# Layer 0's attention scores as one-pass products of halves, two units in a batch

## The chip, the cores and the metric

The kernel runs on one core of a Trainium2 chip. The metric is the time of one execution in microseconds of device time, median over runs; a profile is one further execution recorded by the hardware profiler, and its span is the time from its first to its last instruction. The engines are TensorE (PE: matmuls; PEld is its weight load), VectorE (DVE), ScalarE (ACT), GpSimd (POOL) and SyncE (SP, which here issues nearly all DMA transfers, in program order).

## The reference

The input is `x`, 8 images of 384 channels by 32 x 32 pixels. Two layers follow each other; the change is in layer 0 alone, an attention over the 1024 pixels of each image with 8 heads of 48 channels and a bias that depends on the distance of two pixels:

```python
tokens = x.reshape(b, c, n).transpose(0, 2, 1)
qkv = (tokens @ qkv_w + qkv_b).reshape(b, n, 3, NUM_HEADS, HEAD_DIM)
qkv = jnp.transpose(qkv, (2, 0, 3, 1, 4))
q, k, v = (qkv[0], qkv[1], qkv[2])
scale = HEAD_DIM ** (-0.5)
attn = jnp.einsum('bhnd,bhmd->bhnm', q * scale, k)
attn = attn + _relative_bias(h, w, mlp_w1, mlp_b1, mlp_w2, mlp_b2)[None]
attn = jax.nn.softmax(attn, axis=-1)
out = jnp.einsum('bhnm,bhmd->bhnd', attn, v)
out = out.transpose(0, 2, 1, 3).reshape(b, n, c)
out = out @ proj_w + proj_b
```

Layer 0 is `x + conv_attention(group_norm(x))`. Layer 1, an attention with 6 heads and a feed-forward part with sign weights, takes its output token by token; nothing in it changes.

## The kernel before

**Order of work.** `_layer0` (L275) runs image after image. For each image the attention's 32 units are followed by the projection of the next image to its queries, keys and values. A scheduler isn't used: every engine runs the instructions in the order in which the Python code writes them, and a small list, `_Later` (L69), runs small pieces of side work a given number of units later. SP's transfers wait in one queue: a transfer whose data isn't there holds back all behind it. The built program gives them eight completion semaphores in turn.

**Pairs.** The 8 heads are 4 pairs. A head pair takes 128 partitions, two halves of 64 rows (`S0`), of which a head fills 48 (`D0`). The 16 rows left over in pairs 0 to 2 (`FR` each) carry the heads of pair 3 (`NF0`): the projection makes three tiles of 128 rows, and six 16-row transfers a side (L680) collect pair 3's rows into its own tile.

**Projection** (`Ahead`, L624). The product with the weights is cut into three one-pass products of parts (`xh` high, `xl` low, `xd` mixed; type fp32r) instead of one four-pass fp32 product; the weights' parts `wc` are read from DRAM in blocks of 576 KB (`_Cut.load`, L161). There are six blocks (`BLOCKS`: 3 pairs, queries or keys), each 18 matmuls of 128x128 by 512. `take` (L666) puts a block's two PSUM tiles together: ACT scales and shifts one (L671), DVE adds the other (L675). After the third block `project_v` makes the values (L700, L708, L712). The order of the six blocks alternates between images, so that three of six weight blocks are already in SBUF for the next image.

**Attention.** A unit is a head pair, 512 of the queries and 256 of the keys. `scores` (L741) makes eight fp32 matmuls on four 64x64 tiles of PE (rows by head, columns by half of the keys), into two PSUM tiles; DVE adds the bias out of PSUM (L759), ACT takes the exponential (L763). `weigh` (L769), two units later (`LAG`), multiplies the exponentials with the values, also in 64x64 tiles, accumulating four units in one PSUM tile; ACT copies its first part (L787) and DVE adds the second (L790). A row of ones beside the values gives the sums. `divide` (L796) sends the sums through DRAM, POOL takes their reciprocals as a power (L808), and `rd`, `rb` (L812, L820) spread them; POOL multiplies (L824). For pair 3 six transfers then move rows back under pairs 0 to 2 (L834). At unit 3 of the next image `project_out` (L860) multiplies with the output weights (`pp`, L847) and adds the residual `res` (L863).

**PSUM.** One pool of four tiles of two banks (`mm2`) serves everything; a tile that is allocated waits until the earliest freed one has been read.

**Beside the units.** Loading the next image, its statistics (`group_norm`), masks of its high parts (`xm`, in the `qk` tiles) and their rounding to `xh`, and cutting layer 1's weights into parts (images 1 to 3) are placed at fixed units.

Of the kernel before, what the change touches and what calls it, by code (L numbers as in the profile page):

```python
# [101 lines left out]
BLOCKS = [(pair, s) for pair in range(KC) for s in range(2)]  # L102
BLOCKS1 = [(0, 1), (0, 0), (1, 1), (2, 1), (1, 0), (2, 0)]
# [171 lines left out]
def _layer0(tc, ins, x1, sums, shared, weights, beside):  # L275
# [9 lines left out]
    with ExitStack() as ctx:  # L285
        const = ctx.enter_context(tc.tile_pool(name="a_const", bufs=1))
        qkp = ctx.enter_context(tc.tile_pool(name="a_qk", bufs=NP0))
# [273 lines left out]
        def project_qk(b, xn):  # L561

            qk = {
                pair: qkp.tile([P, 2, N], F32, tag="qk", name=f"qk{b}_{pair}") for pair in range(NP0)
            }
            for pair in range(NF0):
                t = qk[pair]
                for s in range(2):
                    pq = mm2(f"pq{b}_{pair}_{s}")
# [11 lines left out]
                    if s == 0:  # L581
                        nc.vector.tensor_scalar(
                            t[:, s], flat2(pq), bias, D0**-0.5, ALU.add, ALU.mult
                        )
                    else:
                        nc.scalar.activation(t[:, s], flat2(pq), AF.Identity, bias=bias)
                    later.step()
                for j in range(2):
                    nc.sync.dma_start(
                        qk[NF0][j * S0 + pair * FR : j * S0 + (pair + 1) * FR],  # L590
                        t[j * S0 + D0 : (j + 1) * S0],
                    )
            return qk

        BB = len(BLOCKS) // 2
# [28 lines left out]
        class Ahead:  # L624
# [4 lines left out]
            def __init__(self, b, xn):  # L629
                self.b, self.xn = b, xn  # L630
                self.qk = {}
                self.parts, self.ps = [[], [], []], {}

            def tile(self, pair):
                if pair not in self.qk:
                    self.qk[pair] = qkp.tile([P, 2, N], F32, tag="qk", name=f"qk{self.b}_{pair}")
                return self.qk[pair]

            def high(self, k):
                return self.tile(k // 2)[:, k % 2]  # L640

            def mask(self, k):
                _masked(nc, self.high(k), self.xn[:, k])

            def round(self, k):
                t = etile(f"xh{self.b}_{k}", dtype=F32R)
                nc.scalar.copy(t, self.high(k))
                self.parts[0].append(t)

            def low(self, k):  # L650
                t = etile(f"xl{self.b}_{k}", dtype=F32R)
                nc.vector.tensor_sub(t, self.xn[:, k], self.high(k))
                self.parts[1].append(t)

            def mixed(self, k):
                t = etile(f"xd{self.b}_{k}", dtype=F32R)
                _mixed(nc, t, self.parts[1][k].bitcast(F32), self.high(k))
                self.parts[2].append(t)

            def products(self, cuts, n, i):  # L660
                if (n, i // 2) not in self.ps:
                    pair, s = BLOCKS[n]
# [3 lines left out]
            def take(self, n):  # L666
                pair, s = BLOCKS[n]
                t = self.tile(pair)[:, s]
# [9 lines left out]
                last = self.tile(NF0)  # L678
                for j in range(2):
                    nc.sync.dma_start(  # L680
                        last[j * S0 + pair * FR : j * S0 + (pair + 1) * FR, s],
                        t[j * S0 + D0 : (j + 1) * S0],
                    )
                later.step()

# [55 lines left out]
        def scores(b, qk, u, weigh):  # L741
            pair, h, m2 = u
            s = [mm2(f"s{b}_{pair}_{h}_{m2}_{j}") for j in range(2)]
            for i in range(2):
                for c in range(2):
                    for j in range(2):
                        rows = slice(j * S0, j * S0 + D0)
                        nc.tensor.matmul(  # L748
                            s[j][ts(c, QP), i], qk[pair][rows, 1, ts(4 * m2 + 2 * i + c, QP)],
                            qk[pair][rows, 0, ts(h, HALF)], start=True, stop=True,  # L750
# [18 lines left out]
        def weigh(b, u, es):  # L769
# [24 lines left out]
            return finish  # L794

# [131 lines left out]
        for k, at in enumerate(((17, 22, 23), (21, 25, 26), (27, 30, 31))):  # L927
            for when, stage in zip(at, cut_weights_v(k)):
                later.after(when + 1, stage)
        for b in range(B):  # L930
            held = []
            for i, u in enumerate(units):
                done = held.pop(0) if len(held) == LAG else None
                held.append(
                    (u, scores(b, qk, u, lambda: weigh(b, *done) if done else None))
                )
                if i == (16 if b == 0 else 1) and b + 1 < B:
                    xn = load(b + 1)
                    for at, stage in zip(
                        (2, 3, 4, 6, 9, 10, 11) if b == 0 else (5, 6, 7, 10, 13, 13, 13),  # L940
# [3 lines left out]
                if i == 3 and b > 0:  # L944
                    project_out(b - 1, residuals(b - 1, etile), range(NF0))
# [5 lines left out]
                if i == 28 and b == 0:  # L951
                    cuts = _Cut(
                        nc, cut, BLOCKS,
                        shared.pool.tile([P, KC * 3 * C], F32R, tag="w", name="wc"),
# [3 lines left out]
                if b in (1, 2, 3) and i == 12:  # L958
                    t = cut_tile(f"cw{b}")
                    weights.load_part(b - 1, t)  # L960
                    for at, stage in enumerate(
                        weights.cut(
                            b - 1, t, lambda name, b=b, t=t: t if name == "cl" else cut_tile(f"{name}1{b}")
                        )
                    ):
                        later.after(4 + at, stage)
                masks, rounds = ((28, 29, 31), ()) if b == 0 else ((25, 26, 27), (28, 29, 30))
                if b + 1 < B:
# [4 lines left out]
                    if i in rounds:  # L973
                        ahead.round(rounds.index(i))

            def weigh_held():
                finish = weigh(b, *held.pop(0))
                if finish is not None:
                    finish()

            if b + 1 == B:
                while held:
                    weigh_held()
                break
            order = [n % len(BLOCKS) for n in range(b % 2 * BB, b % 2 * BB + len(BLOCKS))]

            if b == 0:
                wh = const.tile([P, KC, C], F32R, tag="wv", name="wvh")
                nc.sync.dma_start(wh.bitcast(F32), cut_v[:, 0])
# [1383 lines left out]
```

## Time and profile before

| | |
|---|---|
| median of 3 runs | 2942.41 us (2942.0 to 2945.76) |
| the profiled execution | 2940.6 us |
| its span | 2939.1 us, mean granted PE clock 0.999 |
| one image, from its projection to the end of its attention | 853.5 to 1019.4 us: 165.9 us, PE busy 165.9, DVE 113.0, ACT 80.2, POOL 26.0 |
| one image later in its cycle, 725.6 to 891.5 us | 165.9 us, PE busy 165.9 |
| HBM read / written | 161.83 / 40.28 MB |

In the busy-time table, the time of the matmuls is a union: several that run side by side count once, and their ends are modelled, so the distance from start to start tells more than a duration. fp32 matmuls leave two records each, one-pass ones a single record. The idle time behind a group names the engine that ended it. In the windows' table each stretch has the busy time of each engine and the number of its instructions.

### The profile page before, as it was taken

How to read it: one execution, taken by the hardware profiler on the slowest of the kernel's cores; microseconds unless marked ns; L12 is line 12 of the kernel's file. 1: busy time of each engine (PE TensorE's matmuls, PEld its weight loads, DVE VectorE, ACT ScalarE, POOL GpSimd, SP SyncE). 2: the span in 40 equal slices, each digit the busy share in tenths (PEclk: the TensorE clock that was granted, in tenths of full speed). 3: DMA queues.
4: the chain of work that ended last, by engine and by line, in shares of the span. 5: the costliest groups of instructions: out<-in, count | busy, mean ns of one | idle time of the engine just before them, and what ended most of it. 6: DMA issues, size and time to landing. Idle time of an engine off the chain costs nothing.

```text
span 2939.1 us, 47521 instructions
## 1 busy us (share of the span) xinstructions
PE 2913.6 (99%) x19538; PEld 1703.0 (58%) x19538; DVE 1969.8 (67%) x1999; ACT 1504.5 (51%) x1846; POOL 493.5 (17%) x318
## 2 busy tenths in 40 slices
PE   8999999999999999999999999999999999999998
PEld 3465665657575666634546647647647647655553
DVE  3976758586676757573655775875875875875756
ACT  2644636264444636363643655555555555564644
POOL 3121202021110202012202202302302302311020
PEclk9999999999999999999999999999999999999999
DMA  7642131413122130323311212112112112112111
GB/s 191 197 147 84 50 111 46 121 45 98 47 74 73 39 113 24 100 69 107 78 56 31 84 31 72 67 32 72 67 32 72 67 32 72 67 40 83 40 46 39
DMA packets 131970, 214.35 MB, mean 73 GB/s; under 512 B 62144, under 2 KB 81072, under 8 KB 130368
## 3 DMA queue, kind: packets, MB, share of 16 engines
q1 hardware_dynamic: 128480, 209.39, 24.3%
q8 instruction: 157, 2.57, 0.4%
q10 hardware_dynamic: 3264, 1.82, 0.2%
q14 instruction: 69, 0.57, 0.1%
HBM read 161.83 MB, written 40.28 MB: 69 GB/s over the span
## 4 chain that ended last, share of the span: by engine, by line
PE 92%; DVE 3%; DMA 2%; ACT 2%; issue 1%; SPq 0%; POOL 0%; DVEq 0%; ACTq 0%
PE s L748 15%; PE o L779 15%; PE s L1725 11%; PE o L1774 10%; PE pg L170 6%; PE y2p L2019 6%; PE y1p L1968 5%; PE pp L847 4%; PE pv L1662 4%; PE pm L170 3%; PE pp L1871 3%; PE vg L700 2%; PE pq L1514 2%; PE pq L572 1%; DMA rb<-rd 1%
## 5 line engine op out<-in xcount | busy, mean ns | idle before, releaser
L763 ACT ACTIVATE e<-e 128x1024 f32<-128x1024 f32 x512 | 534.5, 1057 | 333.2 <-DVE e L759 316.7
L759 DVE TENSOR_TENSOR e<-s,grow 128x1024 f32<-128x1024 f32 x512 | 601.1, 1218 | 154.6 <-PE s L748 137.8
L748 PE MATMUL s<-qk 48*64 48x512 f32 x4096 | 606.4, 590 | 1.8 <-DVE e L759 1.8
L779 PE MATMUL o<-e,v 64*64 64x512 f32 x4096 | 603.5, 589 | 0.0
L1736 ACT ACTIVATE e<-s,kc 128x512 f32<-128x512 f32 x768 | 463.3, 693 | 173.5 <-PE s L1725 163.9
L1725 PE MATMUL s<-qk,qk 64*64 64x512 f32 x3072 | 419.4, 592 | 1.6 <-DVE oT L1784 1.3
L1774 PE MATMUL o<-e,v 64*64 64x512 f32 x3072 | 415.0, 590 | 0.0
L748 PEld LDWEIGHTS s<-qk 48*64 48x64 f32 x4096 | 231.7, 132 | 235.3 <-issue 98.7
L779 PEld LDWEIGHTS o<-e,v 64*64 64x64 f32 x4096 | 251.6, 133 | 188.4 <-issue 97.3
L1725 PEld LDWEIGHTS s<-qk,qk 64*64 64x64 f32 x3072 | 154.3, 132 | 191.5 <-issue 109.0
L1751 DVE TENSOR_TENSOR t<-t,e 128x1024 f32<-128x1024 f32 x192 | 230.9, 1221 | 45.6 <-ACT e L1736 45.4
L1774 PEld LDWEIGHTS o<-e,v 64*64 64x64 f32 x3072 | 160.5, 133 | 168.2 <-issue 141.9
L808 POOL TENSOR_TENSOR inv<-sums,over 128x16 f32<-128x16 f32 x32 | 95.8, 2992 | 843.9 <-DMA sums<-sd 776.8
L1955 DVE TENSOR_REDUCE parts<-y 128x1 f32<-128x1024 f32 x75 | 89.7, 1217 | 102.6 <-ACT y L1952 102.1
L1748 DVE TENSOR_TENSOR t<-e,e 128x1024 f32<-128x1024 f32 x96 | 114.0, 1224 | 58.8 <-ACT e L1736 58.7
L1631 POOL TENSOR_TENSOR hc<-hc,rsqrt 128x32 f32<-128x32 f32 x24 | 136.7, 5696 | 2.0
L1662 PE MATMUL pv<-wv,bx 128*128 128x384 f32 x384 | 128.3, 491 | 0.0
L1871 PE MATMUL pp<-oT,L_attn_proj_wT 128*128 128x512 f32 x288 | 126.3, 595 | 1.9 <-DVE oT L1837 1.8
L847 PE MATMUL pp<-oT,wp 128*128 128x512 f32 x288 | 125.7, 595 | 0.0
L1662 PEld LDWEIGHTS pv<-wv,bx 128*128 128x128 f32 x384 | 119.4, 314 | 9.8 <-ACT e L1736 4.1
L675 DVE SCALAR_TENSOR_TENSOR qk<-pg,qk 128x1024 f32<-128x1024 f32 x42 | 51.4, 1225 | 100.3 <-PE pg L170 74.2
L1968 PE MATMUL y1p<-lun,w 128*128 128x512 f32 x360 | 113.5, 396 | 3.0 <-DVE lun L1918 3.0
(225 smaller groups left out, 3583.8 us busy)
## 6 DMA issues: line engine op xcount, KB each, us to landing
rb<-rd SPq DMA_DIRECT2D x110, 256.0 KB
wc<-there SPq DMA_DIRECT2D x25, 576.0 KB
wc<-cut SPq DMA_DIRECT2D x24, 576.0 KB
xn<-in_x_dram SPq DMA_DIRECT2D x24, 512.0 KB
res<-in_x_dram SPq DMA_DIRECT2D x24, 512.0 KB
x<-res SPq DMA_DIRECT2D x24, 512.0 KB
bx<-x SPq DMA_DIRECT2D x8, 1536.0 KB
rq<-hi SPq DMA_DIRECT2D x48, 256.0 KB
```

Source lines behind the costliest of these rows:

```text
L170: self.nc.tensor.matmul(out[:, h], w[:, i, k], part[k][:, ts(h, HALF)], start=(k == 0 and i != 1), stop=(k == KC - 1 and i != 0),)
L748: nc.tensor.matmul(s[j][ts(c, QP), i], qk[pair][rows, 1, ts(4 * m2 + 2 * i + c, QP)], qk[pair][rows, 0, ts(h, HALF)], start=True, stop=True,)
L759: nc.vector.tensor_add(e.rearrange("p (i q) -> p i q", i=2), s[j], bass.AP(near.tensor, near.offset, [near.ap[0], [-QROWS * IW, 2], [1, HA ...
L763: nc.scalar.activation(e, e, AF.Exp)
L779: nc.tensor.matmul(po[ts(j, S0), r], v[keys, 2 * m2 + i, 2 * pair + j, :], es[j][keys, ts(i, HALF)], start=(m2 == 0 and i == 0), stop=(m2 ...
L847: nc.tensor.matmul(pps[b, m][:, h], (wp[:, k] if k < NF0 else wl)[:, ts(m, P)], oT[:, k, ts(h, HALF)], start=(k == 0), stop=(k == (NF0 if ...
L1662: nc.tensor.matmul(pv[:, i, 0:C], xt[:, k].rearrange("c (p m) -> c m p", m=MT)[:, 2 * m2 + i], wv[:, k], start=(k == 0), stop=(k == KC - 1),)
L1725: nc.tensor.matmul(s[j][ts(c, QP), i], qk[pair, 1][rows, ts(4 * m2 + 2 * i + c, QP)], qk[pair, 0][rows, ts(h, HALF)], start=True, stop=True,)
L1736: nc.scalar.activation(e[:, ts(i, HALF)], s[j][:, i], AF.Exp, scale=kc[:, pair, j, m : m + 1])
L1751: nc.vector.tensor_add(total[j], total[j], e)
L1774: nc.tensor.matmul(po[ts(j, D1), r], v[keys, 2 * m2 + i, at : at + D1], es[j][keys, ts(i, HALF)], start=(m2 == 0 and i == 0), stop=(m2 == ...
L1968: nc.tensor.matmul(py[m][:, h], w1[:, k, ts(m, P)], un[k][i][:, ts(h, HALF)], start=(k == 0 and i == 0), stop=(k == KC - 1 and i == 1),)
```

## The change

For images 1 to 7 (image 0 keeps its way):

- **Halves.** Each block of queries or keys is split after `take` into a high part, rounded to fp32r by an ACT copy, and the rest, by a DVE subtraction. From these, one-pass products are put together that use all 64 rows: `PIECES` says which rows of which part lie where. A query is two tiles (high 0-47 and rest 0-15; rest 16-47 twice), a key three; the products (query 0, key 0), (0, 1), (1, 2) sum to high x high, high x rest, rest x high and rest x rest over 48 channels.
- **Where they come from.** Blocks are taken in the order `BLOCKS0`, pair 0's keys first. Pair 0's tiles are put together by transfers inside SBUF (`move`); only its 16 left-over rows go to DRAM (`keep_rows`). The other pairs' parts are stored whole in DRAM (`there`) and loaded in pieces one pair ahead (`load_k`, `load_q`). Pair 3's rows are gathered from DRAM by the same loads.
- **Batches.** Two units are one batch: four score tiles of 128 keys by two heads by 512 queries, each six one-pass matmuls (K = 64, M = 128) on two row halves of PE; then the sums of the batch before, 8 fp32 matmuls (K = 128, M = 64) on two column halves in a PSUM tile of their own. The first batch of a pair's 512 queries is copied out by ACT, the second added by DVE.
- **Moved.** The roundings go from beside the last units to behind them; the statistics come at other units; `wc` is loaded anew for each image at unit 26 (all six blocks instead of three); the residuals are loaded at the end of the projection, into the buffer of `wc`, and layer 1's weights are cut there too. The `qk` pool is eight tiles of 128 x 1024 instead of four of twice that size.

The diff, cut to its core:

```diff
+BLOCKS0 = [(0, 1), (0, 0), (1, 1), (1, 0), (2, 1), (2, 0)]
...
+        PIECES = [
+            (((0, D0, 0, 0), (D0, FR, 1, 0)), ((0, 2 * FR, 1, FR), (2 * FR, 2 * FR, 1, FR))),
+            (((0, D0, 0, 0), (D0, FR, 1, 0)), ((0, D0, 1, 0), (D0, FR, 0, 0)),
+             ((0, 2 * FR, 0, FR), (2 * FR, 2 * FR, 1, FR))),
+        ]
...
             def take(self, n):
...
-                last = self.tile(NF0)
-                for j in range(2):
-                    nc.sync.dma_start(
-                        last[j * S0 + pair * FR : j * S0 + (pair + 1) * FR, s],
-                        t[j * S0 + D0 : (j + 1) * S0],
-                    )
                 later.step()
+                def halves():
+                    if not here or s == 1:
+                        nc.scalar.copy(high, t)
+                        nc.vector.tensor_sub(rest, t, high.bitcast(F32))
+                    if here and s == 1:
+                        self.keep_rows(s, pair, (high, rest), slice(0, N))
+                        self.move(pair, 1, self.k[pair], (high, rest))
+                    elif not here:
+                        for x, part in enumerate((high, rest)):
+                            nc.sync.dma_start(self.there[s, pair, x], part.bitcast(F32))
+                    for h in range(NH if here and s == 0 else 0):
+                        up, part = self.q_tiles(pair, h)[0], t[:, ts(h, HALF)]
+                        nc.scalar.copy(up, part)
+                        nc.vector.tensor_sub(part, part, up.bitcast(F32))
+                        self.keep_rows(s, pair, (up, part), ts(h, HALF))
+                        self.move(pair, 0, self.q[pair, h], (up, part))
+                return halves
+
+            def keep_rows(self, s, pair, parts, cols):
+                for x, part in enumerate(parts):
+                    for j in range(2):
+                        rows = slice(j * S0 + D0, (j + 1) * S0)
+                        nc.sync.dma_start(
+                            self.there[s, pair, x, rows, cols], part[rows].bitcast(F32)
+                        )
+            def move(self, pair, s, tiles, parts):
+                pieces = PIECES[s]
+                for to, of in reversed(list(zip(tiles, pieces))):
+                    for row, n, x, at in of:
+                        if row == at and to is parts[x]:
+                            continue
+                        for j in range(2):
+                            nc.sync.dma_start(
+                                to[j * S0 + row : j * S0 + row + n].bitcast(F32),
+                                parts[x][j * S0 + at : j * S0 + at + n].bitcast(F32),
+                            )
+            def load(self, to, s, pair, cols, pieces):
+                for row, n, x, at in pieces:
+                    for j in range(2):
+                        rows = to[j * S0 + row : j * S0 + row + n].bitcast(F32)
...
+                        nc.sync.dma_start(rows, of)
...
+        class Batches:
...
+            def weigh(self):
+                pair, h, g, es = self.held
...
+                po = mm2(f"o{self.b}_{pair}_{h}_{g}")[:, 0]
+                for i in range(BT):
+                    for j in range(2):
+                        nc.tensor.matmul(
+                            po[ts(j, S0)], v[:, BT * g + i, 2 * pair + j, :],
+                            es[i][:, ts(j, HALF)], start=(i == 0), stop=(i == BT - 1),
+                        )
...
+            def run(self, n, between):
...
+                def products(i):
+                    ss.append(mm2(f"s{name}_{i}"))
+                    for m, (a, c) in enumerate(((0, 0), (0, 1), (1, 2))):
+                        for j in range(2):
+                            nc.tensor.matmul(
+                                ss[i][:, j], k[c][ts(j, S0), ts(BT * g + i, P)],
+                                q[a][ts(j, S0)], start=(m == 0), stop=(m == 2),
+                            )
...
+                for i in range(3):
+                    products(i)
+                take(0)
+                products(3)
+                for i in range(1, 4):
+                    take(i)
+                finish = self.weigh() if self.held else None
+                self.held = pair, h, g, es
+                between()
+                if finish is not None:
+                    finish()
...
+                    def between(n=n):
+                        pair, at = divmod(n, 4)
+                        if at == 0:
+                            if pair > 0:
+                                halves.load_q(pair, 1)
+                            if pair < NF0:
+                                halves.load_k(pair + 1)
+                        elif at == 2 and pair < NF0:
+                            halves.load_q(pair + 1, 0)
...
+            def take(n):
+                halves = ahead.take(n)
+                if n < BB:
+                    cuts.load(n + BB)
+                if n == BB - 1:
+                    ahead.project_v(0)
+                halves()
```

## The prediction

> **What bounds the kernel now.** I read the page's engine line and the chain that ended last, then the busy time of one image (853.5 to 1019.4 us) in its stages.
>
> ```profile
> PE 2913.6 (99%) x19538; PEld 1703.0 (58%) x19538; DVE 1969.8 (67%) x1999; ACT 1504.5 (51%) x1846; POOL 493.5 (17%) x318
> PE 92%; DVE 3%; DMA 2%; ACT 2%; issue 1%; SPq 0%; POOL 0%; DVEq 0%; ACTq 0%
> ```
> ```profile
> 853.50:891.40 37.90, 37.90 (x182) 32.55 (x180) 19.04 (x26) 7.29 (x7) 5.28 (x2) 1.00 0.45 121
> 891.40:902.85 11.45, 11.45 (x98) 4.75 (x97) 9.72 (x9) 6.70 (x7) 0.00 (x0) 1.00 0.74 248
> 902.85:918.50 15.65, 15.65 (x40) 6.76 (x38) 3.31 (x3) 1.76 (x2) 0.00 (x0) 1.00 0.24 96
> 918.50:1019.40 100.90, 100.90 (x930) 59.18 (x929) 80.93 (x77) 64.44 (x66) 20.70 (x13) 1.00 0.09 23
> ```
> The columns are length, PE, PEld, DVE, ACT, POOL, clock, DMA share, GB/s. PE is full in all four: projection (37.9), the first four units (11.45), output projection (15.65), 28 units (100.9); 165.9 in all. Any PE idle time is therefore paid, and any PE work saved is a gain. The PE timeline prices the work:
>
> ```profile
> 887.12 1.56 PE L170 MATMUL pm<-xd,wc 128*128 128x512 f32 x6
> 888.52 1.56 PE L170 MATMUL pg<-xh,wc 128*128 128x512 f32 x6
> ...
> 902.85 15.72 PE L847 MATMUL pp<-oT,wp 128*128 128x512 f32 x36
> 918.49 1.95 PE L748 MATMUL s<-qk 48*64 48x512 f32 x16
> 920.26 1.90 PE L779 MATMUL o<-e,v 64*64 64x512 f32 x16
> 921.98 1.90 PE L748 MATMUL s<-qk 48*64 48x512 f32 x16
> ```
> ```profile
> 1486.45 1.92 PE L1801 MATMUL sum<-f,ones 128*32 128x512 f32 x16
> 1488.31 1.95 PE L1725 MATMUL s<-qk,qk 64*64 64x512 f32 x16
> ```
> Starts are what counts. A one-pass matmul of 512 columns takes 1.40/6 = 0.233 us. An fp32 one is two records; four 64x64 tiles run side by side, 16 records in 1.72 us, 0.43 a step. Column tiles of 128 rows (L1801) keep that step: 16 records in 1.86 with two changes of tile form. 902.85 + 15.64 against 36 x 0.43 = 15.48, and 918.49 to 920.26 (1.77) against 1.72, show about 0.09 us for a change of form.
>
> **Part 1: scores and sums.** A batch is two units, before 4 x 1.72 = 6.88 us. Its 24 score matmuls now have K = 64, M = 128, one pass: 12 pairs on two row halves. No row shows such a pair, so its step p is bounded: 0.214 (half the fp32 step) if one-pass row tiles stream like an fp32 pass, 0.466 (2 x 0.233) if they don't overlap. The nearest row, L748, overlaps row tiles without loss, so I take 0.235, the one-pass step. Scores 12 x 0.235 = 2.82; sums 16 records in two column tiles, 8 x 0.43 = 3.44; two changes 0.18: 6.44. In the last stage stand 14 batches of scores and 15 of sums: 39.5 + 51.6 + 28 x 0.09 = 93.6 against 100.9. DVE has 4 adds at 1.16 (row L759, 6 in 6.88) and an oT add of 0.69, 5.3 of 6.44; batches with statistics or masks spill some 0.4 an image. **Gain 6.9 us an image** (10.4 at 0.214; a loss of 31.9 at 0.466).
>
> The L748 rows show four tiles in the time of one. The page "TensorE: Matmul & The Clock Gate", section "Measured speedup vs the span model", gives only 3.07 for four row tiles; scaled to two this would be 1.53, p = 0.304, and the total 7 x 11.6 us higher.
>
> **Part 2: the projection, read from SP.** Times here run from the projection's start (853.50 = 0), with the waits of the built program.
>
> ```profile
> 863.19 1.18 SPq L680 DMA_DIRECT2D qk<-qk  x2
> 864.46 0.54 SPq L161 DMA_DIRECT2D wc<-cut  x1
> ...
> 869.59 1.12 SPq L820 DMA_DIRECT2D rb<-rd  x2
> 870.81 0.53 SPq L161 DMA_DIRECT2D wc<-cut  x1
> ...
> 877.07 3.98 SPq L834 DMA_DIRECT2D oT<-oT  x6
> ```
> A 16-row transfer inside SBUF holds SP 0.57 us (1.18 for 2, 3.98 for 6; median of L680 0.561); a full 128-row store 0.34 to 0.42. In the trace's landing records it lands after 2.3, a store of 512 KB after 2.6, rb after 4.0, a wc block after 4.4 to 6.5.
>
> Before, SP has 59 transfers an image, now 174. Two per block go (L680, 12); 84 loads, 32 for the first pair, 8 stores and 3 wc loads come. In the projection the order is now: wc(3), 12 K transfers, rd, rb, wc(4), 20 Q transfers, wc(5), 6 oT, then the stores of the other pairs. Worked through:
> - Block 0's ACT take ends at 8.4, DVE's at 9.65 (as before). New: ACT copy 1.03 (row L647), DVE subtraction 1.22 (row L652), to 12.0. DVE and ACT wait for each other meanwhile, which PE's four buffers just hide.
> - The K transfers go out 11.1 to 18.1, rd 18.1, rb 19.6 (behind rd's landing, 1.5), wc(4) 20.7.
> - 20 Q transfers x 0.57 = 11.4, and 1.2 for the eighth-last transfer's landing (SP has eight semaphores in turn; wc(4) lands at 26.5): 33.9. They land at 35.7.
> - wc(5) leaves at 33.9 and lands at 38.7. PE wants it for block 5 at 35.1 (0.4 later than before for the rounding now behind the last exps, 0.5 for a v buffer, and the rest as before), so it idles 3.6 and more; block 5 ends at 43.0 against 37.9.
>
> **Part 3: the start of the scores.**
>
> ```profile
> 891.59 1.23 DVE L675 SCALAR_TENSOR_TENSOR qk<-pg,qk 128x1024 f32<-128x1024 f32 x1 [2.98 <-PE pg L170]
> 893.41 6.88 DVE L759 TENSOR_TENSOR e<-s,grow 128x1024 f32<-128x1024 f32 x6 [0.60 <-PE s L748]
> ```
> Before, the first add follows the last take at 39.9. Now DVE and ACT come late, in order: block 3's tile is the one that the Q moves read, so its take waits for 35.7; its copy needs the buffer of block 2's stored half, which goes out behind the oT transfers (37.9, landed 40.5); blocks 4 and 5 follow, each about 3.7 long (take 1.23, copy 1.03, subtraction 1.22, gaps). DVE is through at 50.2. The first batch has no sums beside it, and the first sums need a fifth buffer, freed by the fifth add: 50.2 + 5 x 1.16 = 56.0, + 3.53 sums = 59.6, where the output projection begins; before, 37.9 + 11.45 = 49.35. **Loss of parts 2 and 3 together: 10.3 us an image.** With SP at 0.35 a transfer and wc at 4.4 the same path gives 4.2; at 0.63 and 6.5 about 13.5.
>
> That landing hides behind nothing shows in L680 and L834. "DMA: Bandwidth & Descriptors", section "Rules for kernel authors", says two transfers to disjoint partition halves serialize and should be one; here each row half has its own. By it the 32 would be 16, and parts 2 and 3 would lose, as an estimate, about 5.
>
> **Costed at nothing.** The loads of pairs 1 to 3 leave two batches (13 us) ahead; 28 transfers x 0.57 = 16 us, and sd, sums, rd, rb some 8 (rd waits for POOL's 2.99 us power), fit in a pair's 26, barely. wc's reload (3 x 576 KB) leaves five units ahead of its use; without that cover it would cost one landing, 4.4 to 6.5, an image. res is issued at the end of the projection (52) and first used at 65; xn follows and is read at 75. The weights cut beside images 1 to 3 and the residuals only change buffers: the w tile is free when each is loaded, and wc waits for the last of them well before its use. A load that comes late stops PE at the first score of its pair, and with it the adds on DVE and the exps on ACT behind it.
>
> **Sum.** Seven projections and seven attentions change: 7 x (10.3 - 6.9) = +24 us. The profiled run took 2940.6 (span 2939.1 and 1.5 around it), so 2964.4; the runs' median, 2942.41, is 1.8 higher: 2966.
>
> **Rivals.**
> - *SP keeps up* (faster). Place: the projection's list; price 4.2 at 0.35 a transfer instead of 10.3. For: x<-res rows take 0.34. Against: those have 128 rows; 16-row rows take 0.57. 7 x (4.2 - 6.9) = -19: 2923. It decides once parts 2 and 3 cost under 6.9, at some 0.44 us a transfer.
> - *Loads late*: pair p + 1's first q stands behind rd and POOL's power and lands around 27 us into a pair of 26. For: the sum above. Against: the eight-deep pipeline may be quicker. Some 2.5 us on two pairs: 7 x 5 more, 3001.
> - *Row tiles don't overlap*: 7 x (11.2 + 31.9) = +302: 3244. For: no row of one-pass tiles. Against: L748.
>
> **Numbers.** Likeliest 0.62 (own range 2942, at p = 0.214, to 2988, at 13.5), SP keeps up 0.20, loads late 0.12, no overlap 0.06. The range 2923 to 3003 leaves out the last and the tails. A difference under 0.2% (6 us) can't be told from none: faster 0.22, same 0.09, slower 0.69.
>
> **What would show it.** Score pairs about 0.235 apart and sum steps 0.43; PE idle before block 5, waiting on wc, and again at the start of the scores, waiting on DVE; 16-row transfers 0.57 apart on SP; the last stage near 94 us. Wrong if that stage stays near 100, if PE waits for q at pairs 2 and 3, or if the projection keeps 38 us.

## The result and the profile after

The changed kernel takes 3149.92 us (median of 4 runs, 3146.82 to 3152.6) against 2942.72 before (4 runs): a ratio of 1.0702, 95% interval 1.0683 to 1.072. It is 207 us slower, where +24 was forecast. The profiled run has a span of 3147.7 us and a mean granted clock of 0.964 (before 2939.1 and 0.999).

The engine line and the clock row in its 40 slices, from the page, then PE's four largest waits from the view of waits (us in total, times, longest):

```profile
PE 2923.4 (93%) x16850; PEld 1673.7 (53%) x16850; DVE 2010.9 (64%) x2048; ACT 1555.8 (49%) x1895; POOL 494.0 (16%) x318
PEclk9999899998999989899899999999999999999999
```
```profile
PE s L920 <- DMA q<-halves: 129.6, 21, 16.0
PE pm L171 <- DMA wc<-cut: 37.0, 7, 6.3
PE s L920 <- DVE e L927: 17.9, 14, 3.0
PE s L920 <- ACT t L681: 12.3, 8, 3.4
```

PE is no longer full: 224 us of the span are idle, and six slices show a clock between 0.8 and 0.9. Two kinds of wait were foreseen: wc before block 5, and DVE and ACT at the start of the scores. The largest was not in the sum, only in a rival: q, 21 waits of which three fall on each of seven images.

One image, cut where PE's work changes (columns: length, busy time of PE, PEld, DVE, ACT, POOL, clock, DMA share, GB/s):

```profile
976.54:1010.70 34.16, 34.12 (x164) 29.17 (x162) 19.60 (x27) 6.52 (x8) 5.30 (x2) 1.00 0.52 138
1010.70:1017.03 6.33, 0.00 (x0) 0.03 (x1) 1.23 (x1) 1.11 (x1) 0.00 (x0) 0.88 0.64 175
1017.03:1023.82 6.79, 6.79 (x18) 5.08 (x19) 2.45 (x2) 2.28 (x3) 0.00 (x0) 0.61 0.76 288
1023.82:1040.13 16.31, 11.90 (x65) 6.27 (x64) 12.73 (x11) 11.09 (x11) 0.00 (x0) 0.90 0.83 278
1040.13:1055.78 15.65, 15.65 (x39) 6.76 (x37) 2.57 (x2) 1.05 (x2) 0.00 (x0) 1.00 0.77 229
1055.78:1121.05 65.27, 65.27 (x401) 32.32 (x400) 54.70 (x53) 43.98 (x44) 10.06 (x9) 1.00 0.36 98
1121.05:1133.73 12.68, 0.07 (x2) 0.03 (x1) 0.00 (x0) 0.71 (x2) 2.90 (x1) 0.65 0.10 29
1133.73:1144.84 11.11, 6.69 (x24) 4.35 (x24) 3.55 (x3) 2.12 (x2) 2.40 (x1) 0.50 0.34 98
1144.84:1171.65 26.81, 26.81 (x153) 12.07 (x152) 21.88 (x22) 18.54 (x19) 5.31 (x2) 0.99 0.30 95
```

The image takes 195.1 us, before 165.9. From the projection's start to the output projection it needs 63.6 (before 49.35), the output projection 15.65 as before, the last stage 115.9 (before 100.9). In that last stage one gap stands out, from 1121.05 to 1144.84: 23.8 us for 24 score records that take 2.94 elsewhere, so 20.8 lost. Without it the stage would be 95.0, a gain of 5.9. So the image pays 14.2 at the start of the scores and 20.8 in the gap, and gains 5.9: 29.1, and seven images 204.

PE around the gap, then SP's list in the same stretch:

```profile
1114.52 3.01 PE L920 MATMUL s<-q,k 64*128 64x512 f32 x24
1117.46 3.65 PE L893 MATMUL o<-e,v 128*64 128x512 f32 x16
1133.73 1.38 PE L920 MATMUL s<-q,k 64*128 64x512 f32 x4 [12.61 <-DMA q<-halves]
1138.90 0.79 PE L920 MATMUL s<-q,k 64*128 64x512 f32 x1 [3.80 <-DMA q<-halves]
1140.31 4.60 PE L920 MATMUL s<-q,k 64*128 64x512 f32 x19 [0.62 <-DMA q<-halves]
```
```profile
1068.56 5.47 SPq L751 DMA_DIRECT2D k<-halves  x12
1078.63 0.52 SPq L955 DMA_DIRECT2D sd<-oT  x2
...
1098.51 11.05 SPq L751 DMA_DIRECT2D k<-halves  x12
1110.54 2.68 SPq L955 DMA_DIRECT2D sd<-oT  x2
1123.12 0.34 SPq L957 DMA_DIRECT2D sums<-sd  x1
1127.85 0.34 SPq L962 DMA_DIRECT2D rd<-inv  x1
1128.29 5.01 SPq L751 DMA_DIRECT2D q<-halves  x8
```

The first row of SP is the loads of K for the third pair, the third row those of the fourth. Both are 12 transfers of 1.5 MB in all. The third pair's pass SP in 5.47 us and land 3.1 to 4.1 us after issue (by the trace's records of semaphore updates); the fourth's take 11.05 and land after 6.5 to 13.8. Behind them sd, 4 KB, lands after 12.4 and 10.1 instead of 1.3. So sums leave at 1123.1, rd at 1127.85, and the fourth pair's first q, next in SP's list, at 1128.3, when PE had been waiting since 1121. The cause is in what the DMA engines did. The view of DMA from 1068.6 to 1078 (K of the third pair), then from 1099 to 1122 (K of the fourth): GB/s in 40 slices, then packets, MB, share of 16 engines:

```profile
GB/s 201 79 200 79 262 174 261 401 279 244 192 244 140 157 227 279 262 279 174 174 244 244 209 140 227 262 244 244 331 209 349 122 122 0 66 13 0 0 0 0
q1 hardware_dynamic: 1076, 1.72, 79.8%
```
```profile
GB/s 114 25 18 28 192 107 71 78 157 157 64 85 78 71 78 85 71 78 86 71 78 85 71 71 57 43 57 57 43 57 57 43 57 57 43 57 57 43 57 57
q1 hardware_dynamic: 524, 1.64, 21.0%
```

The fourth pair's rows moved at some 76 GB/s, then 52, with a fifth of the engines' time in use; the third pair's at 220 in the mean of the slices in which they ran. 76 is three times 25, 52 is twice 26. The fourth pair's heads lie in DRAM as 16 rows in each of three pairs, so its loads read three pairs (or two) outermost, then 16 rows: 4 x 192 KB at 76 GB/s are 10.3 us, 4 x 128 KB at 52 are 10.1, 20.4 of the 24.2 between the first issue (1098.5) and the last landing (1122.7). The records of semaphore updates tell the number of engines apart from any rate. Each of the third pair's K loads leaves 16 updates. Of the fourth pair's, each with three pairs outermost leaves 4, each with two pairs 3; sd leaves 2. In these one update comes early (0.4 to 1.2 us after issue) and then 3, 2 or 1 follow.

The Trainium skill's page "DMA: Bandwidth & Descriptors", section "Why a DMA increments its semaphore by 16 and not by 1", says that a transfer uses the largest number of engines up to 16 that divides the outermost dimension above 1 of both sides, and the lowest-numbered ones: 3 or 2 here, 16 where the outermost is 48 or 32 rows, and 1 for a single row such as sd, behind the others on the same engine. The rates and the updates agree with 3, 2 and 1. Which engines they were the trace doesn't tell, but the order of landing fits shared ones: the fourth pair's four loads of a single pair's 16 rows, 64 KB each and with all 16 updates, land only after 7.5 to 10.6 us, each within 0.5 us of the slow load ahead of them.

### The profile page after: what moved, and what is told of

It is laid out like the page before. It is cut to its first block, busy times and chain, and to the rows that moved or that the text cites. A ratio compares the mean times of both kernels' runs of the same rounds, so it can differ in the third digit from the quotient of the medians.

```text
span 3147.7 us, 43577 instructions
## 1 busy us (share of the span) xinstructions
PE 2923.4 (93%) x16850; PEld 1673.7 (53%) x16850; DVE 2010.9 (64%) x2048; ACT 1555.8 (49%) x1895; POOL 494.0 (16%) x318
## 4 chain that ended last, share of the span: by engine, by line
PE 45%; DVE 3%; DMA 2%; ACT 1%; issue 1%; SPq 0%; POOL 0%; DVEq 0%; ACTq 0%
PE s L1903 10%; PE o L1952 10%; PE y2p L2197 5%; PE y1p L2146 4%; PE pv L1840 4%; PE pp L2049 3%; PE pg L171 2%; PE pq L1692 1%; PE pm L171 1%; DVE qk L1773 1%; DMA rb<-rd 1%; PE sum L1979 1%; PE pp L997 1%; PE hs L1788 1%; PE o L893 1%
## 5 line engine op out<-in xcount | busy, mean ns | idle before, releaser
L931 ACT ACTIVATE e<-e 128x1024 f32<-128x1024 f32 x448 | 473.6, 1058 | 408.0 <-DVE e L927 386.1
L927 DVE TENSOR_TENSOR e<-s,grow 128x1024 f32<-128x1024 f32 x448 | 517.8, 1216 | 215.2 <-PE s L920 208.9
L920 PE MATMUL s<-q,k 64*128 64x512 f32 x2688 | 381.2, 425 | 161.8 <-DMA q<-halves 129.6
L920 PEld LDWEIGHTS s<-q,k 64*128 64x128 f32 x2688 | 264.2, 198 | 314.7 <-issue 140.5
L1952 PE MATMUL o<-e,v 64*64 64x512 f32 x3072 | 414.4, 590 | 0.0
L893 PE MATMUL o<-e,v 128*64 128x512 f32 x1792 | 409.6, 600 | 0.3 <-DVE e L927 0.3
L1952 PEld LDWEIGHTS o<-e,v 64*64 64x64 f32 x3072 | 159.4, 133 | 169.3 <-issue 142.2
L893 PEld LDWEIGHTS o<-e,v 128*64 128x64 f32 x1792 | 120.0, 137 | 236.5 <-issue 218.1
L2133 DVE TENSOR_REDUCE parts<-y 128x1 f32<-128x1024 f32 x75 | 89.7, 1217 | 102.8 <-ACT y L2130 102.3
L171 PE MATMUL pm<-xd,wc 128*128 128x512 f32 x392 | 113.0, 429 | 37.0 <-DMA wc<-cut 37.0
L974 POOL TENSOR_TENSOR oT<-oT,rb 128x1024 f32<-128x1024 f32 x32 | 76.6, 2394 | 321.7 <-DMA rb<-rd 266.0
```

Of the source, the lines that this page charges most:

```text
L171: self.nc.tensor.matmul(out[:, h], w[:, i, k], part[k][:, ts(h, HALF)], start=(k == 0 and i != 1), stop=(k == KC - 1 and i != 0),)
L893: nc.tensor.matmul(po[ts(j, S0)], v[:, BT * g + i, 2 * pair + j, :], es[i][:, ts(j, HALF)], start=(i == 0), stop=(i == BT - 1),)
L920: nc.tensor.matmul(ss[i][:, j], k[c][ts(j, S0), ts(BT * g + i, P)], q[a][ts(j, S0)], start=(m == 0), stop=(m == 2),)
L927: nc.vector.tensor_add(e.rearrange("p (j q) -> p j q", j=2), ss[i], near(2 * pair, BT * g + i, h, [GW * IW, 2]),)
L931: nc.scalar.activation(e, e, AF.Exp)
L1952: nc.tensor.matmul(po[ts(j, D1), r], v[keys, 2 * m2 + i, at : at + D1], es[j][keys, ts(i, HALF)], start=(m2 == 0 and i == 0), stop=(m2 == ...
```

## The experiments

Each is timed against runs of the kernel before that stand beside it (2941.8 to 2943.9 us from group to group, so a gain taken between two groups can be off by 2 us); the last two columns come from its profiled run's PE timeline (mean over the images 1 to 7 of the time from the projection's start to the output projection; mean over images 1 to 6 of the last stage).

| run | us | ratio (95% interval) | to output projection | last stage |
|---|---|---|---|---|
| before | 2942.7 | 1 | 49.4 | 100.9 |
| changed | 3149.9 | 1.0702 (1.0683 to 1.072) | 62.9 | 117.2 |
| e1_rows_first | 3000.6 | 1.0196 (1.0179 to 1.0213) | 62.9 | 95.6 |
| e2_rows_first_k | 3047.7 | 1.0356 (1.0339 to 1.0373) | 62.6 | 102.8 |
| e3_rows_first_wc | 3010.4 | 1.023 (1.0212 to 1.0247) | 64.6 | 95.1 |
| e4_rows_first_act | 2987.6 | 1.0148 (1.0131 to 1.0164) | 61.2 | 95.6 |
| e5_k_pool | 2978.1 | 1.0128 (1.0112 to 1.0145) | 59.5 | 95.6 |
| e6_full_keep | 2992.3 | 1.0171 (1.0154 to 1.0188) | 62.9 | 95.5 |
| e7_q_last | 3013.8 | 1.0245 (1.0228 to 1.0262) | 65.2 | 95.3 |
| e8_all | 2990.7 | 1.0166 (1.0149 to 1.0183) | 61.9 | 95.6 |
| e9_moves_pool | 2973.9 | 1.0107 (1.0091 to 1.0122) | 59.3 | 95.5 |
| e10_all_moves_pool | 2962.8 | 1.0068 (1.0054 to 1.0082) | 57.2 | 96.0 |
| e11_stores_first | 2949.1 | 1.0021 (1.0012 to 1.003) | 55.6 | 95.3 |
| e12_best | 2923.2 | 0.9928 (0.9914 to 0.9942) | 52.1 | 95.4 |

**The outermost dimension.** e1 turns the source round for both loads, and e3 to e12 keep this. e2 turns it for K alone; its fourth pair then multiplies queries and keys whose rows stand in different orders, so its scores there are not the reference's, and it serves for its time only.

```diff
                             of = self.there[
                                 s, at // FR : (at + n) // FR, x, j * S0 + D0 : (j + 1) * S0, cols
                             ]
+                            of = of.rearrange("c r n -> r c n")
```

> The loads of the fourth pair read a source of three (or two) pairs of 16 rows; here the 16 rows come first and the pairs second, so the fourth pair's rows stand in another order, the same for K and Q; number, bytes and order of the transfers stay. Theory A (engine spread: a transfer whose outermost dimension is 3 or 2 runs on 3 or 2 of the 16 DMA engines, and the sums' one-row transfers queue behind it): the fourth pair's K transfers land within 6 us instead of 6 to 14, sd within 3 instead of 10 to 12, PE's wait for q at the fourth pair falls from 17.4 us an image to 0 to 3, mean clock 0.98 or more, time 3149.9 - 7 x (17 to 21) = 3003 to 3031. Theory B (SP has too many transfers, and q stands behind rd and POOL's power): SP's list is the same, so the wait stays above 12 us and the time at 3120 to 3150.

> Only K's loads of the fourth pair have the 16 rows first; Q's keep three (or two) pairs outermost, so scores of the fourth pair pair up rows in different orders (its heads are not the reference's). Theory A: sd lands in time and the fourth pair's first Q loads leave some 12 us earlier, but still take 7 to 12 us on few engines; a wait for q of 3 to 8 us an image is left, and the time lies 7 x (2 to 7) = 15 to 50 above that with both in row order. Theory B: no change against the changed kernel, 3120 to 3150.

e1 is 149.3 us faster than the changed kernel: theory A, and 2 us more than it allowed. Its mean clock is 0.983. The fourth pair's loads in e1, on SP:

```profile
1012.25 7.60 SPq L752 DMA_DIRECT2D k<-halves  x12
1019.95 0.68 SPq L956 DMA_DIRECT2D sd<-oT  x2
1021.95 0.34 SPq L958 DMA_DIRECT2D sums<-sd  x1
1026.49 0.34 SPq L963 DMA_DIRECT2D rd<-inv  x1
1026.92 4.77 SPq L752 DMA_DIRECT2D q<-halves  x8
```

The list is the same, in the same order, but each of the 12 loads of K now leaves 16 updates and lands after 2.6 to 3.9 us, sd lands within 1.8, and PE's wait for q falls from 129.6 us to 1.4 in all. That the list is long, and that q stands behind rd and POOL's power (theory B), costs nothing by then. e2 lies 47.1 us above e1, inside what A allowed and near its end: of the 149, K's form with what queues behind it made 102, Q's own slow loads 47 (PE still waits 31.6 us for q in e2, 4.5 an image).

**Is PE's wait for wc paid?** e3 puts wc(5) in front of Q's 20 transfers.

```diff
                         nc.vector.tensor_sub(part, part, up.bitcast(F32))
-                        self.keep_rows(s, pair, (up, part), ts(h, HALF))
-                        self.move(pair, 0, self.q[pair, h], (up, part))
+
+                def moves():
+                    for h in range(NH if here and s == 0 else 0):
+                        parts = self.q[pair, h][0], t[:, ts(h, HALF)]
+                        self.keep_rows(s, pair, parts, ts(h, HALF))
+                        self.move(pair, 0, self.q[pair, h], parts)
...
                 if n == BB - 1:
+                    held_moves()
                     ahead.project_v(0)
```

(`held_moves` is block 1's `moves`.)

> Both loads in row order, and wc(5) goes out ahead of the 20 Q transfers of the first pair. Theory C (the prediction's part 2: PE's idle time before block 5 is paid): the 6.3 us of idle and the 2.6 us at half clock behind it go, and the time is 7 x (5 to 9) = 35 to 63 below the kernel with row order alone. Theory D (the start of the scores is set by the chain on ACT and DVE: block 3's take waits for the Q moves to land, its copy for the stored half of block 2, which leaves SP behind all Q and oT transfers; PE's idle time lies beside it): PE's wait for wc goes, but output projection still begins some 63 us after the projection's start and the time stays within 7 us of it, rather later, as Q goes out 0.6 us later.

9.8 us slower than e1: theory D, though 3 us beyond its bound. The wait didn't go, it changed its name. PE's first wait in e3:

```profile
PE pm L171 <- ACT t L681: 42.6, 7, 7.2
```

42.6 us instead of 37.8 in e1, at the same place: block 5 needs a PSUM buffer that block 3's take frees, and the take waits for Q's moves, which now leave later. In the changed kernel the two ended together: block 3's take ended at 1016.1, wc(5) landed at 1016.9.

**Where Q's moves stand.** e4 gives Q's 12 moves to ACT's queue, issued behind block 2's copy:

```diff
                         for j in range(2):
-                            nc.sync.dma_start(
+                            (nc.scalar if s == 0 else nc.sync).dma_start(
                                 to[j * S0 + row : j * S0 + row + n].bitcast(F32),
```

e5 gives K's 8 moves to POOL's queue in the same place (`nc.gpsimd if s == 1 else nc.sync`). e6 stores whole tiles:

```diff
                 for x, part in enumerate(parts):
-                    for j in range(2):
-                        rows = slice(j * S0 + D0, (j + 1) * S0)
-                        nc.sync.dma_start(
-                            self.there[s, pair, x, rows, cols], part[rows].bitcast(F32)
-                        )
+                    nc.sync.dma_start(self.there[s, pair, x, :, cols], part.bitcast(F32))
```

e7 puts Q's transfers behind block 2's halves (with `moves` as in e3), and e8 joins e5, e6 and e7:

```diff
                 halves()
+                if n == BB - 1:
+                    held_moves()
```

> Both loads in row order, and the 12 moves of the first pair's Q are issued by ACT, behind its copy of block 2, where it had 19.5 us idle; the 8 stores of Q stay on SP. Theory D: the moves leave at 18 to 26 us after the projection's start instead of 25 to 36, block 3's take comes at 29 to 32 instead of 37.2, the stored half of block 2 leaves SP at 29 instead of 40.3, DVE is through at 42 to 45 instead of 53.9, output projection begins at 51 to 55 instead of 63.6, and the time is 7 x (8.5 to 12.5) = 60 to 88 below the kernel with row order alone. Theory C: only wc(5) leaves earlier, by some 6 us; 35 to 63 below, and output projection begins at 55 to 59.

> Both loads in row order (the base: 3000.6 us, output projection begins 64.2 us after the projection's start), and the 8 moves of the first pair's K are issued by POOL, which is idle there, instead of SP. Theory D1 (SP's list of issues sets when Q's moves land): rd, rb, wc(4) and Q's 20 transfers leave some 6 us earlier, block 3's take comes at 30 to 32 instead of 37, wc(5) is there in time, output projection begins at 55 to 59, and the time is 7 x (5 to 9) = 35 to 63 below the base. Theory D2 (not the issuing but the eight semaphores and the landing of what is in flight hold the list up, as where ACT issued Q's moves and only 2 us an image came of it): 0 to 15 us below the base.

> Both loads in row order, and the first pair's rows for the packed pair are kept by storing the whole tile instead of two groups of 16 rows: 2 stores of K instead of 4, 4 of Q instead of 8, all 128 rows. D1 (number of issues): 6 transfers x 0.57 = 3.4 us an image less on the chain, 12 to 28 us below the base. Rival (bytes: 3 times 512 KB more to HBM beside the moves): the moves land later and it is 0 to 14 us above the base.

> Both loads in row order, and Q's 20 transfers stand behind wc(5) and behind block 2's two stored halves, so that block 3's tile takes a buffer of those and block 4's take is the one that waits for Q to land. If the order of release decides: block 3's take comes at 27 to 29 instead of 37, its stored halves still leave behind Q and oT (40 to 42), block 4 and 5 follow; DVE is through 2 to 4 us earlier, 14 to 28 us below the base, and PE does not wait for wc. If the landing of Q alone decides: Q lands 1.4 us later and it is 5 to 15 us above the base, as with wc(5) alone ahead.

> All four together: row order, K's moves from POOL, whole-tile stores of the first pair, Q's transfers behind wc(5) and block 2's stores. D1: Q leaves at 20 to 29 us and lands at 31, DVE is through at 42 to 45 instead of 54, output projection begins at 51 to 55 instead of 64.2; an image takes 162 to 166 us, before 165.9, and the time is 2915 to 2945. D2: little beyond the parts, 2965 to 2990.

None did in full what it was to do. e4 gained 13 us where 60 to 88 were expected. ACT in e4, around its idle stretch:

```profile
1070.01 1.05 ACT L692 CAST th<-t 128x1024 fp32r<-128x1024 f32 x1 [1.29 <-DVE t L685]
1070.02 17.80 ACTq L728 DMA_DIRECT2D q<-t  x12
1089.29 1.11 ACT L681 ACTIVATE t<-pm,bq 128x1024 f32<-128x1024 f32 x1 [18.22 <-DMA q<-t]
```

Twelve transfers took 17.8 us instead of 7. Four go at once; the fifth overwrites rows of q that SP still has to store, and those stores stand in SP's list behind rd, rb and wc(4), whose issues end at 1076.8 in this image. e5 gained 22.5, between D2's 15 and D1's 35. e6 gained 8, between D1's 12 and the rival's nothing; its profiled run took 2999.8, as long as e1's and 7.5 above its own median, so its stage times say nothing on that gain, and it stays open whether fewer and larger stores are better. e7 lost 13, inside the 5 to 15 that its second alternative, the landing of Q alone, allowed. SP in e7:

```profile
918.22 1.27 SPq L162 DMA_DIRECT2D wc<-cut  x2
924.28 3.71 SPq L989 DMA_DIRECT2D oT<-oT  x6
928.09 0.53 SPq L699 DMA_DIRECT2D halves<-th  x1
928.72 0.38 SPq L699 DMA_DIRECT2D halves<-t  x1
929.14 2.06 SPq L717 DMA_DIRECT2D halves<-q  x2
```

Block 2's stores, and Q's transfers with them, now stand behind oT's moves, which wait for POOL's product until 924.3, and SP stands still with them from 919.5. e8, at the upper edge of D2's 2965 to 2990, inherits that. So the chain of theory D stands, but D1's link in it, the number of transfers that SP issues, explains only a part (e5's 22.5 us); in e4 and e7 it is what each transfer stands behind.

**Taking the links out.** e9 has POOL issue all moves of K and Q; e10 oT's too; e11 lets the stores of 16 rows go ahead of weights, rd and rb.

```diff
-                            nc.sync.dma_start(
+                            nc.gpsimd.dma_start(
                                 to[j * S0 + row : j * S0 + row + n].bitcast(F32),
...
-                            nc.sync.dma_start(
+                            nc.gpsimd.dma_start(
                                 oT[j * S0 : j * S0 + SP, c], oT[row : row + FR, pair]
```
```diff
                 halves = ahead.take(n)
+                halves()
                 if n < BB:
                     cuts.load(n + BB)
                 if n == BB - 1:
                     ahead.project_v(0)
-                halves()
```

(The first pair of lines is e9, the second e10, the second diff e11, which also moves `later.step()` from the take to the end of `halves`.)

> Both loads in row order (base 3000.6 us), and all 20 moves of the first pair's K and Q inside SBUF are issued by POOL (0.49 us each there, and its own semaphores), SP keeps the 12 stores of 16 rows. With K's alone the time was 2978.1 and Q's still left SP until 32 us after the projection's start, behind rb's landing. If the place of Q's moves in SP's list sets the start of the scores: Q lands at 27 to 29, block 3's take comes as soon as PE has its sums (28.6), wc(5) is there in time (PE waits under 1 us), output projection begins at 51 to 55 and the time is 2915 to 2950. If what is in flight sets it (the weights of block 4, rb and the stores share the DMA engines), Q lands at 31 to 33 from whatever queue, output projection begins at 57 to 60 and the time is 2970 to 2985.

> The same, and the 6 moves of oT go to POOL too, behind the product there that they wait for. SP then has nothing that waits for POOL between wc(5) and block 2's stored halves: these leave 3 to 4 us earlier (at 24 to 27 instead of 27 to 31), block 3's copy does not wait for them, output projection begins at 50 to 54, and the time is 0 to 25 us below that with oT's moves on SP, 2905 to 2945. If PE's own work up to block 5 (38.2 us) and the takes, copies and subtractions behind it bound the start, it is within 7 us of it.

> All moves on POOL as in the run before (2962.8 us), and the stores of 16 rows, which POOL's moves wait for because they overwrite the rows stored, go out ahead of wc(4), rd and rb instead of behind them; a block's weights are loaded after its halves. In the run before these stores left 19 to 25 us after the projection's start beside 576 KB of weights and 512 KB of rb and took 4 to 6.5 us to land, and POOL's last 8 Q moves left at 26.4 to 30.4. If that is what holds block 3's take (at 34.8): the stores leave at 15 to 19 and land within 2.5, POOL's moves are out by 24, the take comes when PE has its sums (29), output projection begins at 50 to 54, an image takes 161 to 165 us (before 165.9), and the time is 2905 to 2942. If the landing is slow whatever stands beside it, it stays at 2955 to 2965.

e9 fell to the second theory's lot (2970 to 2985). e10 gained 11 more, inside its 0 to 25, but the output projection began at 57.2 and not at 50 to 54. e11 gained another 14, not the 20 to 58 expected. POOL in e10 and in e11:

```profile
884.77 1.98 POOL L725 DMA_DIRECT2D q<-t  x4
892.70 3.96 POOL L725 DMA_DIRECT2D q<-t  x8 [5.95 <-DMA halves<-q]
```
```profile
1043.76 1.99 POOL L725 DMA_DIRECT2D q<-t  x4
1046.29 3.97 POOL L725 DMA_DIRECT2D q<-t  x8 [0.54 <-issue]
```

The wait of 5.95 us for the stores of q is gone in e11, so that link is shown; how much of the 14 us is its own is not, as e11 also moves the loads of weights. What was left there: block 2's stored halves, behind rb and wc(4), landed 7 to 8.4 us after issue, and ACT waited for them before block 3's take.

**A version below both.** e12 goes on from e11: rd and rb two steps later, so that wc(4) and block 2's stores leave first, and the last block's copy, subtraction and stores, with the loads of the second pair's K, only in the second batch. The values of the first rows (`project_v(0)`) come ahead of block 2's halves again.

```diff
-            later.after(2, keep_inverse)
+            late = 2 if pair == NF0 and b + 1 < B else 0
+            later.after(2 + late, keep_inverse)
...
-                            if pair < NF0:
+                            if 0 < pair < NF0:
                                 halves.load_k(pair + 1)
+                        elif n == 1:
+                            last_halves()
+                            halves.load_k(1)
```

> On top of the run before (2949.1 us; output projection begins 55.4 us after the projection's start, 49.35 before the change): wc(4) and block 2's stored halves leave ahead of rd and rb, rd and rb two steps later; the values of the first two rows of tiles are formed ahead of block 2's copy again; the copy, subtraction and stores of the last block wait until the second batch, and the loads of the second pair's K with them. If the start of the scores is set by DVE's chain behind the takes, and that by the landing of stored halves beside rb and wc: stored halves land within 5 us instead of 8, the takes follow PE without waits, DVE begins the adds 3 to 6 us earlier (at 40 to 43 instead of 46), output projection begins at 49.5 to 53, an image takes 160 to 163.5 us and the time is 2905 to 2931, below both kernels. If the work put off comes back in the first batches (sums late behind DVE, the second pair's K late), the last stage grows by what the start gains and the time stays at 2940 to 2950.

2923.2 us, ratio 0.9928 (0.9914 to 0.9942): 20 us below the kernel before, 227 below the changed one. One image of e12, start of the scores, output projection, last stage:

```profile
844.34:895.92 51.58, 48.66 (x247) 37.93 (x245) 34.77 (x40) 19.59 (x21) 18.20 (x28) 1.00 0.72 228
895.92:911.57 15.65, 15.65 (x40) 6.76 (x38) 3.79 (x3) 2.27 (x3) 0.00 (x0) 1.00 0.93 264
911.57:1006.37 94.80, 94.80 (x577) 46.40 (x577) 79.98 (x77) 65.36 (x66) 20.73 (x13) 1.00 0.41 110
```

162.0 us an image. The put-off work didn't come back: the last stage stays at 95.

## Why the prediction was right or wrong

The step that failed is the one under "Costed at nothing": the loads of pairs 1 to 3 were put at no cost, and the fourth pair's cost 149 of the 207 us. The parts that were worked out are 34 us short together.

- **Part 1, the batches: right.** The step of a score pair is (2.94 - 0.09) / 12 = 0.2375 us, taken at 0.235. In the undisturbed stretch a batch takes 6.52 to 6.53 from start to start, forecast 6.44: sums take 3.58 with their change of form, the rest is as worked out. The last stage without its gap is 95.0 to 95.6 instead of 93.6, the gain 5.3 to 5.9 an image instead of 6.9. The third rival (no overlap, 3244) is out, and the factor of 3.07 from the page "TensorE: Matmul & The Clock Gate", section "Measured speedup vs the span model", which scaled to two tiles would have made p 0.304, doesn't hold here.
- **Part 2, wc(5): the times nearly right, what they cost wrong.** The moves inside SBUF left SP 0.56 to 0.63 us apart while it had no other wait, the 16-row stores, priced alike, 0.34 to 0.56. wc(5) left at 35.9 us after the projection's start (forecast 33.9) and landed at 40.4 (38.7); PE stood 6.3 us (3.6 and more). Not foreseen was the lower clock behind it: 18 records took 6.79 us, at 0.61 in the mean, instead of 4.2. But e3 shows that this idle time is not the price: without it PE waits at the same place for ACT.
- **Part 3, the chain through ACT and DVE: right, each link late.** Block 3's take came at 37.2 (35.7), block 2's stored half left SP at 40.3 (37.9), DVE was through at 53.9 (50.2), output projection began at 63.6 (59.6). The loss is 14.2 us in this image, 13.5 in the mean, forecast 10.3. Two terms are mis-sized, by the means over the seven images: SP reaches block 2's stored halves at 39.4 instead of 37.9, wc(5) being 1.1 late already, and DVE needs 13.8 from there instead of 12.3, as the first two stored halves land after 3.0 to 3.9 and some later ones after 4 to 4.8, where I had 2.6 from a quieter stretch. That the mean loss equals the upper case of the prediction, 13.5, is chance: that case took 0.63 a transfer and 6.5 for wc, and wc(5) landed after 4.2 to 4.6. In e10 and e11 landings weigh more: moves wait for stores whose rows they overwrite, and block 2's stored halves land after 5 to 8 us beside weights and rb.
- **"Costed at nothing", the loads of pairs 1 to 3: wrong, and this is the miss.** The step counted 28 x 0.57 = 16 us of issues on SP and found room in a pair's 26. On SP it was even less: a plain load left every 0.46 us. Pairs 1 and 2 never waited. But the step asked only when a load leaves, not how many engines carry it, and the fourth pair's source has another form than the others; it gave no landing time for it at all. Its loads ran on 3 or 2 engines, and its K landed after up to 13.8 us, with sd behind it; this cost 149 of the 207 us (e1).
- **The rival "loads late"** named the place, q behind rd at a pair's start, but with 2.5 us on two pairs and SP's issues as the cause. It was 20.8 us on one pair, and with SP's list unchanged e1 removes it. The sign that the text set for itself, PE waiting for q at pairs 2 and 3, came at pair 3.
- **"SP keeps up" (2923)** did not come true: from start to output projection the changed kernel lost 13.5, not 4.2. e12 reaches that time only with the list rearranged.
- **The rule of "DMA: Bandwidth & Descriptors", section "Rules for kernel authors", on partition halves** (one transfer instead of two) was not tried.

The remainder after e1 adds up: 7 x (13.5 - 5.3) = 57 us, measured 3000.6 - 2942.7 = 58. With the loads at full width the forecast of +24 would have been 34 us short: 7 x 3.2 = 22 from parts 2 and 3, 7 x 1.6 = 11 from the gain of part 1.

## What to carry to other kernels

For each new load, write down the outermost dimension of its source and destination beside its bytes: a transfer whose outermost dimension is the number of heads or pairs may run on that many DMA engines, and whatever small transfer follows queues behind it. A queue's cost is not only its number of issues but also what its head waits for, so list for each transfer the store, product or landing it stands behind. A wait that ends at the same time as another is not worth its own length: e3 removed one of 5.4 us an image and gained nothing.

## What was not expected of the hardware

- Loads with 3 or 2 groups outermost moved 76 and 52 GB/s, some 26 for each group; the third pair's K, as many bytes with 48, 32 or 16 rows outermost, 220. The number of engines shows in a transfer's semaphore updates: 16 for the third pair's K loads, one early update and then 3, 2 or 1 for the narrow ones.
- After the idle stretch of 12.7 us PE's granted clock was 0.50 for the next 11 us: 24 score records were busy 6.69 us instead of 2.94. Of the 20.8 us of a gap, 3.7 are this, as an estimate (6.69 - 2.94). After 6.3 us idle it was 0.61 over 6.8 us. The Trainium skill's page "TensorE: Matmul & The Clock Gate", section "Part 1: The HAM clock gate (the "warmup" mystery)", says that an idle window of some 3.4 us halves the clock until about as long a busy one; the rows agree in kind.
- A 4 KB transfer took 12.4 us instead of 1.3 behind slow loads that it had nothing to do with.
- POOL's queue issues a move inside SBUF every 0.49 us (e10, e11), SP's every 0.56 to 0.63.
